# Convolution in a four-layer kernel: taps spread over four engines, and the transposed result stored by blocks of 32 rows

## The chip, the core and the metric

The kernel runs on one core of a Trainium2 chip, in one launch. The metric is device time in microseconds. A core has a matrix engine (TensorE, PE in the profile), a vector engine (VectorE, DVE), an activation engine (ScalarE, ACT), a general engine (GpSimd, POOL) and a queue that here only issues DMAs (SyncE, SP). They run side by side and wait for each other by semaphores. TensorE writes to PSUM, an accumulator memory of eight banks, each of which holds one 128x512 float32 tile; other data is in SBUF, the on-chip memory with 128 partitions, or in DRAM.

## What is computed

Four layers on an image of 256x256 positions with 128 channels, in float32, each of the form `x = x + layer(group_norm(x))`. The change touches layer 1, a selective state-space scan in four directions. Its start, cut from the reference:

```python
xz = x @ w_in.T
xi, z = jnp.split(xz, 2, axis=-1)                    # xi: 256 inner channels
xc = jnp.transpose(xi, (0, 3, 1, 2))
xc = depthwise_conv3x3(xc, conv_w) + conv_b          # one 3x3 filter per channel
xc = silu(xc)
x_flat = xc.reshape(b, d, L)                         # row by row
x_t = jnp.transpose(xc, (0, 1, 3, 2)).reshape(b, d, L)   # column by column
x_hwwh = jnp.stack([x_flat, x_t], axis=1)
xs = jnp.concatenate([x_hwwh, jnp.flip(x_hwwh, axis=-1)], axis=1)
```

The four sequences in `xs` (by rows, by columns, and both backwards) then each go through a projection, a softplus, and a recurrence over all 65536 positions with 16 states per channel.

## The kernel before

`program` runs a pass for the statistics and then the layers one after the other. Layer 1 (`layer1`) is three stages: `conv_block` (the convolution), `scan_stream` (the scan, by far the longest part of the whole kernel) and `scan_end`.

**The convolution.** The inner channels are two halves of 128 (`dh`), which lie on the partitions. The image is cut into 16 blocks of 16 rows; a block and a half make a *part*, 32 parts in all, numbered `i`. Each part has eight *units* `u` of two rows, so a unit is a tile of 128 channels by 512 positions, and there are 256 units. A unit passes through these steps:

- `products` (line 472): some of the nine taps on TensorE. Since projecting and filtering are both linear, the projection's weights are multiplied by the tap's weights beforehand (`taps`, line 434), and one matrix product from the normalised input `xps` gives projection and tap at once, summed into the PSUM tile `l1a_mm`. A float32 product stands in the trace as two records.
- `rest` (line 487): the other taps on VectorE. Each is one instruction (line 493) that multiplies a shifted window of the projected input `l1a_xi` in SBUF by a weight per channel and adds it to `l1a_mm`.
- `silu` (line 502): two ScalarE instructions read the finished tile, one (line 511) into `l1a_o`, row by row, the other (line 512) into `l1a_ot`, a tile of 256 columns by 32 rows in which neighbouring rows of one column are neighbours.

`on_pe` (line 420) names the taps on TensorE: four of the nine in even units, three in odd ones. So VectorE does five taps or six, in turns.

`inner_x` (line 457) makes `l1a_xi` for the next part: one product with the plain projection weights into `l1a_pi` (two PSUM banks) and one ScalarE copy (line 471) for each of the nine pairs of rows. At its start VectorE clears the borders of a new `l1a_xi` (line 462); there are two such buffers, so that this waits for the last tap of the part before. `load_x` and `norm_x` (lines 439 and 453) bring the next block of input into `l1a_xp`, in two DMAs, and normalise it on VectorE (line 455).

The loop (line 536) writes out the order by hand, and every engine takes its instructions in that order: at unit `n` come `products(n)`, `rest(n-1)`, `inner_x` of the next part, and `silu(n-3)`. The pool of `l1a_mm` has five PSUM banks, so TensorE can be ahead of `silu` by that many units.

**What is stored.** For every 8 rows `l1a_o` goes to the DRAM tensor `l_xc`, by rows, and for every 32 rows `l1a_ot` goes to `l_xct`, by columns (line 521). `l_xct` is laid out as 256 channels by 65536 positions with whole columns in a run, so that 32 rows of a column are a run of 128 bytes, and one store has 32768 of them.

**The scan.** `scan_stream` takes the four directions `k` one after the other, each in 128 chunks of 512 positions. For a pair of chunks one block `l1b_xc` of 1024 positions and both halves is loaded from `l_xc` (k = 0 and 2) or `l_xct` (k = 1 and 3), by one DMA (line 625). It is read by TensorE for the projection (`xproj`, line 643) and, in the first two directions, for the start of the output sum (`y_start`, line 793), and by VectorE in `delta_x` (line 717), which multiplies step sizes in PSUM by `x`. The bulk of a chunk is sixteen recurrences on VectorE (line 769), with products on VectorE and GpSimd (lines 736 and 784), and loads of the spread-out `b` and `c` (lines 663 and 669). The outputs `y` of the directions by columns already have a layout by blocks of 32 rows, `[256, S // 32, S, 32]`; `in_block` and `block_dma` (lines 596 and 604) address such a block, which has runs of 32 elements in SBUF and of 512 bytes in DRAM.

Between convolution and scan stand the loads of the scan's weights (`scan_weights`, line 891); all these DMAs, stores and loads alike, are issued by SP, in the program's order.

Of the kernel before, what the change touches and what calls it, by code (L numbers as in the profile page):

```python
# [413 lines left out]
def conv_block(c, x1, ab, xc, xct):  # L414

    tc, nc, t = c.tc, c.nc, c.t
    R, RO, RT = 16, 8, 32
    on_pe = ((0, 2, 6, 8), (0, 2, 6))  # L420
    NU = R // 2
    parts = [(b, dh) for b in range(S // R) for dh in range(2)]
    with ExitStack() as a:
# [3 lines left out]
        wk = a.enter_context(tc.tile_pool(name="l1a_wk", bufs=2))  # L427
        ps = a.enter_context(tc.tile_pool(name="l1a_ps", bufs=5, space=PSUM))
        psi = a.enter_context(tc.tile_pool(name="l1a_pi", bufs=2, space=PSUM))
# [6 lines left out]
        cb = load(nc, one, t["l1_convb"], "l1a_cb")  # L436
        xps, raw, xis, mms, os_, ots = {}, {}, {}, {}, {}, {}

# [34 lines left out]
        def products(i, u):  # L473
            b, dh = parts[i]
            r = 2 * u
            mm = mms[i, u] = ps.tile([P, 2, S], F32, name="l1a_mm")
            for n, tap in enumerate(on_pe[u % 2]):
                dy, dx = divmod(tap, 3)
                nc.tensor.matmul(
                    mm,  # L480
                    taps[:, tap, dh * P : dh * P + P],
                    xps[b][:, r + dy : r + dy + 2, dx : dx + S],
                    start=n == 0,
                    stop=n == len(on_pe[u % 2]) - 1,
                )

        def rest(i, u):
            dh, r, mm = parts[i][1], 2 * u, mms[i, u]
            for tap in range(9):
                if tap in on_pe[u % 2]:  # L490
                    continue
                dy, dx = divmod(tap, 3)
                nc.vector.scalar_tensor_tensor(  # L493
                    mm,
                    xis[i][:, r + dy : r + dy + 2, dx : dx + S],
                    each[:, dh, tap : tap + 1],
                    mm,
                    ALU.mult,
                    ALU.add,
                )  # L500

        def silu(i, u):
# [17 lines left out]
            if rt == RT - 2:  # L520
                nc.sync.dma_start(
                    xct[ds_].rearrange("p (w h) -> p w h", h=S)[:, :, h1 - RT : h1], ots.pop(dh)
                )

# [9 lines left out]
        for r in range(NU + 1):  # L534
            inner_x(0, r)
        for n in range(len(parts) * NU + 3):
            i, u = divmod(n, NU)
            if i % 2 == 0 and i + 2 < len(parts) and u in (1, 5, 7):
                if u == 1:
                    load_x(parts[i + 2][0])  # L540
                else:
                    norm_x(parts[i + 2][0], u // 7)
            late(products, n)
            late(rest, n - 1)
# [7 lines left out]
def scan_stream(c, xc2, y, w):  # L552
# [18 lines left out]
    with ExitStack() as a:  # L571
# [31 lines left out]

        def block_dma(k, i, yo, store):
            b = i * CH // BL
            if k % 2 == 0:
                pairs = [(y[k][:, bass.ts(b, BL)].rearrange("(h p) t -> p h t", p=P), yo)]
            else:
                pairs = [
                    (  # L610
                        y[k][h * P : h * P + P, :, bass.ts(b, NW)].rearrange("p b w r -> p b (w r)"),
                        yo[:, h].rearrange("p (b m) -> p b m", m=NW * R),
                    )
                    for h in range(2)
                ]
            for far, near in pairs:
                nc.sync.dma_start(*((far, near) if store else (near, far)))

        def load_x(ch):

            if ch >= N:
                return
            k, i = chunks[ch]
            xc = io.tile([P, 2, BL], F32, name="l1b_xc")
            nc.sync.dma_start(
                xc, xc2[k % 2][:, bass.ts(i * CH // BL, BL)].rearrange("(h p) t -> p h t", p=P)
            )
            blocks[ch] = blocks[ch + 1] = [xc, None]

        def load_y(ch):  # L630
# [4 lines left out]
            if k >= 2:  # L635
                block_dma(k - 2, i, yo, False)

        def xproj(ch):
# [3 lines left out]
            for dh in range(2):  # L642
                nc.tensor.matmul(  # L643
                    du1[:40],
                    w["xproj"][:, dh, k, :],
                    blocks[ch][0][:, dh, cols(ch)],
                    start=dh == 0,
# [66 lines left out]
        def delta_x(ch, dh):  # L714
            if ch >= N:
                return
            nc.vector.tensor_tensor(  # L717
                du1 if dh else mm, mm, blocks[ch][0][:, dh, cols(ch)], ALU.mult
            )
# [67 lines left out]
        def y_start(ch, dh):  # L787
# [4 lines left out]
            else:  # L792
                nc.tensor.matmul(
                    ys[dh], w["dsum"][:, k, dh], xc[:, dh, cols(ch)], start=True, stop=False
                )
# [11 lines left out]
        def y_out(ch, dh):  # L807
# [3 lines left out]
            yo = blocks[ch][1]  # L811
            got = ys[dh] if k % 2 == 0 else ys[dh].rearrange("p (w b r) -> p w b r", b=S // R, r=R)
            nc.scalar.copy(in_block(yo, ch, dh), got)
            if dh == 1 and ch % 2 == 1:
                block_dma(k, i, yo, True)

# [282 lines left out]
def layer1(c, x1, x2p, x2, ab, stats):  # L1099
    tc = c.tc  # L1100
    with ExitStack() as ctx:
        dram = ctx.enter_context(tc.tile_pool(name="l1_dram", bufs=1, space=DRAM))
        xc = dram.tile([256, NPOS], F32, name="l1_xc")
        xct = dram.tile([256, NPOS], F32, name="l1_xct")
        shapes = [256, NPOS], [256, S // 32, S, 32]
        y = [dram.tile(shapes[k % 2], F32, name=f"l1_y{k}") for k in range(4)]
        conv_block(c, x1, ab, xc, xct)
# [612 lines left out]
```

## Time and profile before

| | us |
|---|---|
| three timed runs, median (lowest to highest) | 34541.69 (34539.79 to 34548.45) |
| the profiled execution's own time | 34537.54 |
| its span, first to last instruction | 34535.8 |
| busy in the span: VectorE, TensorE, GpSimd, ScalarE | 31354.0, 29222.5, 26717.0, 22500.8 |
| convolution, first tap product to last silu | 1146.4 |
| scan, start of the first recurrence to the end of the last | 25569.2 |

The profile is of one execution. It gives, for groups of like instructions, the source line, the engine, the operation, the tile written and the tiles read, shapes, count, busy time and mean length of one in ns, and the idle time before them with what ended it. A wait is put down to the instruction whose semaphore ended it. The granted clock (PEclk) is the share of full speed that TensorE was given in a stretch; in the windows it stands behind the engines' busy times, and DMA behind it is the mean busy share of the 16 DMA engines. A timeline line is start, length, engine, line, operation, and how many like instructions it merges.

### The profile page before, as it was taken

What the parts mean: (1) busy time and instruction counts of PE and PEld (TensorE: products, weight loads), DVE (VectorE), ACT (ScalarE), POOL (GpSimd) and SP (SyncE); (2) the same over time, 40 slices, a digit from 0 to 9 for tenths busy, and PEclk for the clock granted to TensorE, in tenths of its full rate; (3) what the DMA queues carried; (4) which work ended last, traced back from release to release, by engine and by line L of the source; (5) the groups of instructions that cost most, each with busy time, mean ns of one, the idle gap of its engine ahead of it and who ended that gap; (6) DMA issues with size and microseconds to landing.
All of it is one profiled execution on the core that took longest, in us unless ns stands there. A gap on an engine that the chain in (4) does not pass through costs nothing. (4 is left out here: it accounts for less than half of the span.)

```text
span 34535.8 us, 255681 instructions
## 1 busy us (share of the span) xinstructions
PE 29222.5 (85%) x72564; PEld 12231.8 (35%) x72564; DVE 31354.0 (91%) x24089; ACT 22500.8 (65%) x46445; POOL 26717.0 (77%) x6484
## 2 busy tenths in 40 slices
PE   7999888888888888888888888888888888899888
PEld 2554333333333333333333333333333333334444
DVE  5668899999999999999999999999999999863699
ACT  3665577777777777777777777777777777532476
POOL 2441199999999999999999999999999999620000
PEclk8999999999999999999999999999999999999888
DMA  3113655555555555555555555555555555674111
GB/s 136 45 45 99 155 190 190 191 191 191 189 191 191 190 190 192 191 190 191 195 201 200 202 201 199 202 204 200 201 202 200 201 202 202 213 236 147 66 34 33
DMA packets 2367335, 5947.80 MB, mean 172 GB/s; under 512 B 637447, under 2 KB 1639704, under 8 KB 1792086
## 3 DMA queue, kind: packets, MB, share of 16 engines
q1 hardware_dynamic: 2230742, 5864.31, 47.6%
q10 hardware_dynamic: 135168, 67.13, 0.6%
q8 instruction: 572, 9.37, 0.1%
q14 instruction: 853, 6.99, 0.1%
HBM read 5238.41 MB, written 692.58 MB: 172 GB/s over the span
## 5 line engine op out<-in xcount | busy, mean ns | idle before, releaser
L769 DVE TENSOR_TENSOR_SCAN l1b_h<-l1b_da,l1b_state,l1b_db 128x1024 f32<-128x1024 f32 x8192 | 18793.1, 2336 | 596.1 <-ACT l1b_db L758 583.8
L784 POOL TENSOR_TENSOR l1b_hc<-l1b_h,l1b_cc 128x2048 f32<-128x2048 f32 x4096 | 18446.0, 4528 | 329.2 <-DVE l1b_h L769 328.4
L803 PE MATMUL l1b_y<-l1b_hc,ident 128*128 128x512 f32 x32768 | 16052.8, 639 | 1117.9 <-POOL l1b_hc L784 1117.8
L754 ACT ACTIVATE l1b_da<-l1b_dl,l_A 128x512 f32<-128x512 f32 (+1 forms) x16384 | 11297.5, 690 | 3156.7 <-DVE l1b_h L769 2848.5
L803 PEld LDWEIGHTS l1b_y<-l1b_hc,ident 128*128 128x128 f32 x32768 | 6524.5, 205 | 10687.1 <-issue 8157.6
L736 POOL TENSOR_TENSOR l1b_db<-l1b_bb,l1b_dus 128x2048 f32<-128x2048 f32 x1536 | 6966.8, 4536 | 1245.2 <-DMA l1b_bb<-l1b_bc 1245.2
L736 DVE TENSOR_TENSOR l1b_db<-l1b_bb,l1b_du 128x2048 f32<-128x2048 f32 x2048 | 4658.4, 2275 | 35.2
L758 ACT ACTIVATE l1b_db<-l1b_state,l1b_db,l1b_af 128x1 f32<-128x1 f32 x8192 | 3045.1, 372 | 0.0
L675 PE MATMUL l1b_mm<-l1b_xd,l_dtw 41*128 41x512 f32 x2048 | 1374.6, 756 | 1714.1 <-ACT l1b_dus L725 1708.3
L701 PE MATMUL l1b_mm<-l1b_tail,ident 128*128 128x512 f32 x2048 | 1292.2, 717 | 1388.4 <-ACT l1b_tail L695 1388.4
L780 ACT COPY l1b_state<-l1b_h 128x4 f32<-128x4 f32 x4095 | 789.7, 193 | 2433.5 <-DVE l1b_h L769 2433.4
L326 POOL TENSOR_TENSOR l0b_e<-l0b_e,l0b_den 128x1024 f32<-128x1024 f32 x512 | 969.0, 1893 | 1403.0 <-DVE l0b_den L325 784.3
L701 PE MATMUL l1b_mm<-l1b_relu,ident 128*128 128x512 f32 x2048 | 1307.4, 727 | 0.0
L675 PEld LDWEIGHTS l1b_mm<-l1b_xd,l_dtw 41*128 41x128 f32 x2048 | 338.0, 206 | 2528.5 <-ACT l1b_dus L725 2131.4
L725 ACT COPY l1b_dus<-l1b_mm 128x512 f32<-128x512 f32 x512 | 299.6, 585 | 1388.2 <-DVE l1b_db L736 1387.7
L736 DVE TENSOR_TENSOR l1b_db<-l1b_bb,l1b_mm 128x2048 f32<-128x2048 f32 x512 | 1171.5, 2288 | 18.2 <-ACT l1b_dus L725 0.7
L302 DVE CUSTOM_DVE_ANT_0 l0b_e<-l0b_sc,l0b_bias 128x256 f32<-128x256 f32 x2048 | 745.5, 420 | 419.0 <-PE l0b_sc L291 415.7
L701 PEld LDWEIGHTS l1b_mm<-l1b_tail,ident 128*128 128x128 f32 x2048 | 377.1, 207 | 2059.0 <-ACT l1b_tail L695 1814.6
L493 DVE SCALAR_TENSOR_TENSOR l1a_mm<-l1a_xi,l1a_each,l1a_mm 128x512 f32<-128x512 f32 x1408 | 1046.1, 755 | 59.1 <-issue 13.0
L643 PE MATMUL l1b_du<-l1b_xc,l_xproj 128*40 128x512 f32 x2048 | 981.5, 602 | 62.4 <-DMA l_xproj<-in_l_xproj 58.8
L317 ACT ACTIVATE l0b_e<-l0b_e,l0b_top 128x256 f32<-128x256 f32 x2048 | 1012.2, 498 | 1.9 <-DVE l0b_top L302 1.9
L709 ACT COPY l1b_dl<-l1b_mm 128x512 f32<-128x512 f32 x1024 | 587.5, 574 | 524.5 <-DVE l1b_du L717 517.0
(256 smaller groups left out, 28744.8 us busy)
## 6 DMA issues: line engine op xcount, KB each, us to landing
l1b_bb<-l1b_bc SPq DMA_DIRECT2D x2048, 1024.0 KB
l1b_cc<-l1b_bc SPq DMA_DIRECT2D x2048, 1024.0 KB
l1b_xc<-l_xc SPq DMA_DIRECT2D x128, 1024.0 KB
l_y<-l1b_yo SPq DMA_DIRECT2D x128, 1024.0 KB
l1b_xc<-l_xct SPq DMA_DIRECT2D x128, 1024.0 KB
l_y<-l1b_yo SPq DMA_DIRECT2D x256, 512.0 KB
l_xc<-l1a_o SPq DMA_DIRECT2D x64, 1024.0 KB
l_xct<-l1a_ot SPq DMA_DIRECT2D x16, 4096.0 KB
```

Source lines behind the costliest of these rows:

```text
L317: nc.scalar.activation(e[:, i], e[:, i], AF.Exp, scale=-1.0, bias=top[:, i : i + 1], accum_out=den[:, i : i + 1],)
L326: nc.gpsimd.tensor_tensor(e, e, den[:, :, None].to_broadcast([P, 4, S]), ALU.mult)
L493: nc.vector.scalar_tensor_tensor(mm, xis[i][:, r + dy : r + dy + 2, dx : dx + S], each[:, dh, tap : tap + 1], mm, ALU.mult, ALU.add,)
L643: nc.tensor.matmul(du1[:40], w["xproj"][:, dh, k, :], blocks[ch][0][:, dh, cols(ch)], start=dh == 0, stop=dh == 1,)
L675: nc.tensor.matmul(mm, w["dt"][:, chunks[ch][0], dh * P : dh * P + P], xds[ch % 3][0:41], start=True, stop=True,)
L701: nc.tensor.matmul(mm, c.ident, part, start=i == 0, stop=i == 1)
L736: eng.tensor_tensor(db, bbs[g // 2], du[:, None, :].to_broadcast([P, G, CH]), ALU.mult)
L754: nc.scalar.activation(da[:, o + lo : o + hi], dl[:, lo:hi], AF.Exp, scale=w["A"][:, k, dh, n : n + 1])
L758: nc.scalar.activation(first, states[k][:, dh, two : two + 1], AF.Identity, scale=af[:, two : two + 1], bias=first,)
L769: nc.vector.tensor_tensor_scan(h_, a_, d_, states[k][:, dh, one : one + 1], ALU.mult, ALU.add)
L784: nc.gpsimd.tensor_tensor(hc, hs[g], ccs[g // 2], ALU.mult)
L803: nc.tensor.matmul(ys[j % 2], c.ident, hc[:, i], start=False, stop=j // 2 * G + i == 15)
```

## The change

Taps 0, 2 and 6 are on TensorE in every unit. Taps 1 and 7 go to ScalarE in every unit: each is an activation with the identity function and the weight as scale, into a tile of its own in SBUF. Tap 4 goes to GpSimd in even units. GpSimd sums these two or three products into one tile (`l1a_t`), and VectorE, which does the other three or four taps as before, adds that tile to `l1a_mm` once. The new step `three` is called at the head of a unit's turn, for the unit after it. The pool of `l1a_mm` gets a sixth bank.

`l_xct` takes the layout by blocks of 32 rows that `y` has, so that a store of `l1a_ot` writes 32 KB in a run for each channel. In exchange, a block of it is loaded by two DMAs with runs of 512 bytes, and lies in SBUF in runs of 32 elements, which the readers of `l1b_xc` follow.

```diff
-    R, RO, RT = 16, 8, 32
-    on_pe = ((0, 2, 6, 8), (0, 2, 6))
+    R, RO, RT = 16, 8, xct.shape[3]
+    on_pe = 0, 2, 6
+    on_act, on_pool = (1, 7), 4
...
-        ps = a.enter_context(tc.tile_pool(name="l1a_ps", bufs=5, space=PSUM))
+        ps = a.enter_context(tc.tile_pool(name="l1a_ps", bufs=6, space=PSUM))
...
-            for n, tap in enumerate(on_pe[u % 2]):
+            for n, tap in enumerate(on_pe):
...
+        def window(i, u, tap):
+            dy, dx = divmod(tap, 3)
+            return xis[i][:, 2 * u + dy : 2 * u + dy + 2, dx : dx + S]
+
+        def three(i, u):
+            dh = parts[i][1]
+            for j, tap in enumerate(on_act):
+                t_ = sums[i, u, j] = wk.tile([P, 2, S], F32, name=f"l1a_t{j}", bufs=3)
+                nc.scalar.activation(
+                    t_, window(i, u, tap), AF.Identity, scale=each[:, dh, tap : tap + 1]
+                )
+            t_ = sums[i, u] = wk.tile([P, 2, S], F32, name="l1a_t", bufs=3)
+            one_, two = sums.pop((i, u, 0)), sums.pop((i, u, 1))
+            if u % 2 == 0:
+                nc.gpsimd.tensor_scalar(
+                    t_, window(i, u, on_pool), each[:, dh, on_pool : on_pool + 1], None, ALU.mult
+                )
+                nc.gpsimd.tensor_tensor(t_, t_, one_, ALU.add)
+                one_ = t_
+            nc.gpsimd.tensor_tensor(t_, one_, two, ALU.add)
 
         def rest(i, u):
-            dh, r, mm = parts[i][1], 2 * u, mms[i, u]
+            dh, mm = parts[i][1], mms[i, u]
             for tap in range(9):
-                if tap in on_pe[u % 2]:
+                if tap in on_pe or tap in on_act or tap == on_pool and u % 2 == 0:
                     continue
...
                 nc.vector.scalar_tensor_tensor(
...
+                    mm, window(i, u, tap), each[:, dh, tap : tap + 1], mm, ALU.mult, ALU.add
+                )
+            nc.vector.tensor_tensor(mm, mm, sums.pop((i, u)), ALU.add)
...
-                nc.sync.dma_start(
-                    xct[ds_].rearrange("p (w h) -> p w h", h=S)[:, :, h1 - RT : h1], ots.pop(dh)
-                )
+                nc.sync.dma_start(xct[ds_, h1 // RT - 1], ots.pop(dh))
...
+        three(0, 0)
         for n in range(len(parts) * NU + 3):
...
+            late(three, n + 1)
             late(products, n)
             late(rest, n - 1)
...
+        def like_block(ap, ch):
+
+            if chunks[ch][0] % 2 == 0:
+                return ap
+            return ap.rearrange("p (w b r) -> p w b r", b=S // R, r=R)
...
             xc = io.tile([P, 2, BL], F32, name="l1b_xc")
-            nc.sync.dma_start(
-                xc, xc2[k % 2][:, bass.ts(i * CH // BL, BL)].rearrange("(h p) t -> p h t", p=P)
-            )
+            block_dma(xc2[k % 2], k, i, xc, False)
...
-                    blocks[ch][0][:, dh, cols(ch)],
+                    in_block(blocks[ch][0], ch, dh),
...
             nc.vector.tensor_tensor(
-                du1 if dh else mm, mm, blocks[ch][0][:, dh, cols(ch)], ALU.mult
+                like_block(du1 if dh else mm, ch),
+                like_block(mm, ch),
+                in_block(blocks[ch][0], ch, dh),
+                ALU.mult,
             )
...
-                    ys[dh], w["dsum"][:, k, dh], xc[:, dh, cols(ch)], start=True, stop=False
+                    ys[dh], w["dsum"][:, k, dh], in_block(xc, ch, dh), start=True, stop=False
...
-        xct = dram.tile([256, NPOS], F32, name="l1_xct")
         shapes = [256, NPOS], [256, S // 32, S, 32]
+        xc = dram.tile(shapes[0], F32, name="l1_xc")
+        xct = dram.tile(shapes[1], F32, name="l1_xct")
```

## The prediction

> **What bounds the kernel now.** I read the windows first, cut at the borders of the stages that the diff touches: the convolution (first tap product to last silu), the passage from it to the scan, and the scan's four passes, from each pass's first recurrence (L769) to the next's, the last to the end of its last.
>
> ```profile
> core 0: us, PE busy (x) PEld busy (x) DVE busy (x) ACT busy (x) POOL busy (x), PEclk, DMA share, GB/s
> 2952.10:4098.50 1146.40, 1054.55 (x2351) 455.98 (x2349) 1090.36 (x1483) 580.03 (x793) 0.00 (x0) 0.95 0.61 141
> 4098.50:4176.80 78.30, 19.78 (x22) 4.79 (x22) 11.07 (x19) 11.16 (x20) 4.50 (x1) 0.57 0.78 197
> 4176.80:10571.80 6395.00, 5344.10 (x10737) 2091.24 (x10738) 6232.59 (x2946) 4505.84 (x9217) 6307.40 (x1408) 0.92 0.51 190
> 10571.80:16966.80 6395.00, 5349.50 (x10757) 2092.66 (x10757) 6232.49 (x2947) 4503.62 (x9213) 6313.64 (x1409) 0.92 0.52 191
> 23361.90:29746.00 6384.10, 5331.97 (x10721) 2087.19 (x10722) 6224.38 (x2940) 4494.87 (x9194) 6312.00 (x1407) 0.92 0.55 200
> ```
>
> In the convolution VectorE is busy 95% of 1146.4 us, TensorE 92%, ScalarE half, GpSimd not at all. In the scan VectorE (97%) and GpSimd (99%) set the pace. Next the convolution's groups and its waits:
>
> ```profile
> L493 DVE SCALAR_TENSOR_TENSOR l1a_mm<-l1a_xi,l1a_each,l1a_mm 128x512 f32<-128x512 f32 x1408 | 1046.1, 755 | 59.1 <-issue 13.0 <-PE l1a_mm L479 4.5
> L479 PE MATMUL l1a_mm<-l1a_xp,l1a_taps 128*128 128x512 f32 x1792 | 851.5, 617 | 73.3 <-ACT l1a_ot L512 73.3
> L512 ACT ACTIVATE l1a_ot<-l1a_mm,l1a_cb 128x512 f32<-128x512 f32 x256 | 294.7, 1151 | 0.0
> ```
>
> ```profile
> ACT l1a_xi L471 <- DVE l1a_xi L462: 119.0, 16, 8.2
> ACT l1a_xi L471 <- DVE l1a_xp L443: 41.1, 14, 3.5
> DVE l1a_mm L493 <- PE l1a_mm L479: 4.5, 10, 0.6
> ```
>
> VectorE waits for TensorE 4.5 us in all: it is the bound, and the taps on it (5.5 a unit, a unit being one 128x512 tile, 256 units) are what costs. Last the timeline, for start-to-start times, since consecutive instructions overlap:
>
> ```profile
> 3206.67 33.96 DVE L493 SCALAR_TENSOR_TENSOR l1a_mm<-l1a_xi,l1a_each,l1a_mm 128x512 f32<-128x512 f32 x44 [0.29 <-issue]
> ...
> 3147.80 3.60 PE L479 MATMUL l1a_mm<-l1a_xp,l1a_taps 128*128 128x512 f32 x8
> ...
> 5011.35 0.63 ACT L695 ACTIVATE l1b_tail<-l1b_tail 128x512 f32<-128x512 f32 x1
> 5011.89 1.40 ACT L754 ACTIVATE l1b_da<-l1b_dl,l_A 128x512 f32<-128x512 f32 x2
> 5013.22 0.37 ACT L758 ACTIVATE l1b_db<-l1b_state,l1b_db,l1b_af 128x1 f32<-128x1 f32 x1
> ```
>
> Eight units of VectorE taps take 33.96 us, 0.77 each; in the trace a tap following another on its own tile starts 0.79 after it, one on a new tile 0.66 after. Eight TensorE records, four taps, end 3.60 after the first starts: one per 0.43 ((3.60-0.59)/7) at full clock.
>
> **VectorE's part.** It loses two taps a unit and gains one addition: three taps and an addition in even units, four and an addition in odd. The addition reads PSUM and one SBUF tile, as L717 does in the scan: 0.674 long; beginning the next tile's work behind it costs what it costs behind a tap now, about 0.09 less than its length, 0.58 (0.71 if it hides nothing, as L717 in the scan). A unit is 3.5 x 0.79 + 0.58 = 3.35 (3.48), plus the normalisation L455, 32 times 1.52 over 256 units = 0.19, plus memsets 0.02: 3.56, or 911 us (945 with the dearer addition). The same sum for before gives 4.5 x 0.79 + 0.66 + 0.21 = 4.43, 1133 us against the 1146.4 seen, so it holds to about 1%.
>
> **TensorE's part.** Three taps are 6 records, the inner product (9 per 8 units) 2.25: 8.25 x 0.43 = 3.54 us a unit instead of 3.97. All units: 906 us at full clock; at the granted 0.95 of this stage, 954. That is above VectorE's 911, so TensorE becomes the bound.
>
> **ScalarE's part.** It adds two Identity activations a unit, SBUF to SBUF, scaled by a column. Nearest rows: L695 (SBUF to SBUF, next start 0.54 later) and L754 (scaled by a column, into PSUM, 1.33 for two): 0.54 to 0.665. 580 + 512 x that = 856 to 920 us; I take 0.6, 887, nearer the first row because the destination is SBUF. Its order per unit is two Identities, one inner copy, two silus. The 160 us of waits at part starts (119.0 + 41.1) are ScalarE arriving early; busy 77% more, it arrives later, and they shrink.
>
> **GpSimd's part.** One scalar multiply and three additions per pair of units. Per element: L784 4528 ns for 2048 makes 1.13 us for an addition, L191 1195 for 1024 makes 0.60: 4.0 us a pair, 511 us in all. The dearest 128x512 addition in the trace, L961 with strided input, takes 1.56: 4 x 1.56 = 6.2 a pair, still under TensorE's 7.4. So it is hidden. VectorE's last addition is a new wait: on GpSimd's sum, which needs ScalarE's two products. Behind it queue the next unit's taps, the normalisations and the memsets that ScalarE's copies wait for. But the products are issued two units before that addition, about 7 us for 1.3 + 2.9 of work, and buffers are three deep; I cost it at nothing. If the cover were gone, the price would be some 3 us at each of 32 part starts.
>
> GpSimd's work beside VectorE has one price that the trace shows, in the stage after the scan:
>
> ```profile
> 29902.35 1.79 DVE L1004 TENSOR_SCALAR l1c_xn<-l1c_x,ab 128x512 f32<-128x512 f32 x1
> ...
> 29900.83 3.02 POOL L961 TENSOR_TENSOR l1c_y<-l1c_y,l1c_yt 128x512 f32<-128x512 f32 x2 [8.02 <-DMA l1c_y<-l_y]
> ```
>
> That VectorE instruction has a median of 0.548 and took 1.79 while a GpSimd addition ran: up to 1.24 late. L455 is the same operation, so 32 x (0 to 1.13, one GpSimd addition) adds 0 to 36 us to VectorE, making it 911 to 947, still below TensorE. The taps and L717 read one SBUF operand, and L717 keeps 0.674 in the scan beside a GpSimd 99% busy: no price. The Trainium skill's page SBUF — State Buffer, "Who interferes with whom", warns that VectorE's 2-port modes and two-SBUF-input operations lock GpSimd out and are locked out by it, for a whole instruction. Applied to every VectorE instruction it would make the offload pointless; by its own limit to those modes and operand kinds it touches L455 alone.
>
> **The stage.** Three engines end near each other: 954, 911 to 947, 887. With hand-overs 1 to 3% above the largest I take 970 (930, where the clock is granted more, to 1020, where all three hold each other up). 1146.4 - 970 = 176 saved.
>
> **The transposed store.** Its 16 issues stay, with whole 32 KB rows instead of 128-byte runs. In the convolution this hides under VectorE; at the end it shows:
>
> ```profile
> 4099.19 35.40 SPq L48 DMA_DIRECT2D l_xproj<-in_l_xproj  x1
> ...
> 4145.34 0.56 ACT L655 COPY l1b_xd<-l1b_du 40x512 f32<-40x512 f32 x1
> ```
>
> SP is held 35.4 us at the first weight load behind the last store, whose drain runs at a flat 145 GB/s in the DMA view; the scan's first copy comes 46.8 us after the convolution's end. Long rows move at 350 to 430 GB/s in that view, so 4 MB take about 11 us, plus 1 MB of l_xc and some 4 us for loads and first products: copy at 15 to 22 us. Saved 25 to 32; I take 28, and keep 12 (200 GB/s, the slow patches between) to 34.
>
> **The scan.** Passes two and four load l_xct by 512-byte runs in two issues: 128 issues of 0.43 us more on SP, ahead of the b and c loads. The passes already say what such loads cost: the fourth loads and stores y like that, the second stores it, the first does neither, yet passes one and two are equal at 6395.0. Cost nothing, the cover being the prefetch of two chunks; without it, some 1 us x 128. VectorE's L717 reads runs of 32 elements, 512 times. ScalarE's L813 writes that pattern in passes two and four: 146.20 us for 256 instructions, against 145.05 for 254 contiguous ones in pass one, 0.571 each in both. Nothing; upper end in the third rival.
>
> **Sum.** 176 + 28 = 204 off the profiled execution's 34537.5 (span 34535.8): 34334. The median of the runs, 34541.7, lies 4 above: 34338.
>
> **Rivals.**
> *ScalarE takes over and keeps its waits.* For: 920 us at the dearer Identity, and 160 us of waits on VectorE's memset (up to 8.2 each), which is a true dependency. Against: those waits come from arriving early. 920 + 160 = 1080, saving 66 + 28: 34444. Chance 0.09.
>
> *GpSimd pays for alternating operations (slower).* No row of before shows a scalar multiply next to an addition. Two switches a pair; GpSimd decides from 1.7 us a switch ((7.4 - 4.0) / 2), the kernel is slower from 2.6 ((9.0 + 0.2 - 4.0) / 2, 9.0 being the pair now and 0.2 the 28 us shared out). At 4.36, the gap before L191 that the timeline most often puts down to issue, the stage is 128 x (4.0 + 8.72) = 1628: 34338 + 658 = 34996. Against: the only two pool configurations of the whole trace stand ahead of L191, though multiplies, additions and copies follow. Chance 0.05. The skill's GPSIMD Engine Reference, "Instruction dispatch", puts some 6 us on the first call to a freshly loaded kernel; paid at each switch, that would be an estimated 2048 us for the stage, and no row here shows it.
>
> *The strided read costs in the scan.* The dearest stride in the trace is L512 against L511, 1151 against 692 ns for 4-byte steps: 0.46 x 512 = 235 us on VectorE, which has no slack there: 34573, no change. Against: L813. Chance 0.03.
>
> **How the numbers follow.** The forecast has 0.83; its own range is a stage of 930 to 1020, a passage of 12 to 34 and 0 to 15 us of strided reads, 34288 to 34419. To leave out no more than 0.2, the range takes the first rival in: 34290 to 34450. 0.2% of this kernel is 69 us, about what its measurement tells from no change. Forecast and first rival (0.92) are faster by more, less 0.05 for mixtures that fall short: 0.87. Same: the third rival and most of the mixtures, 0.07. Slower: 0.06.
>
> **What would show it.** Right: convolution 930 to 1020 us; TensorE busiest there, with VectorE waiting for l1a_mm from TensorE; Identity pitch 0.54 to 0.67; GpSimd additions near 1.13; first L655 copy 15 to 22 us after the last silu; passes within 2 us of 6395. Wrong: GpSimd above 7 us a pair, ScalarE over 95% busy, VectorE waiting for l1a_t, or a second and fourth pass longer than the first.

## The result, and the profile after

| | before | after |
|---|---|---|
| median of the runs, us (lowest to highest) | 34540.74 (34534.36 to 34548.45) | 34313.07 (34306.94 to 34318.44) |
| ratio, 95% interval | | 0.9934 (0.9921 to 0.9946) |
| the profiled execution's own time, its span | 34537.54, 34535.8 | 34318.44, 34316.7 |
| convolution, first tap product to last silu | 1146.4 | 940.0 |
| from there to the first recurrence | 78.3 | 53.3 |
| four passes of the scan | 25569.2 | 25569.4 |
| from the end of the last recurrence to the end of the span | 4789.7 | 4804.1 |

The kernel became 228 us faster, 0.66%. Between the two profiled executions lie 219.1 us: 206.4 in the convolution, 25.0 in the passage, 2.3 ahead of both, and 14.4 lost again after the scan. That last number is not the change's. The stage after the scan, whose code is the same in all kernels here, took between 1045.3 and 1059.3 us (first to last instruction on a tile of its own) in the eleven executions profiled, and the profile after happens to hold the longest.

The windows of the changed kernel, cut as those of before, so that they can be laid line beside line (the passage is the second row, the first two passes of the scan the last two):

```profile
core 0: us, PE busy (x) PEld busy (x) DVE busy (x) ACT busy (x) POOL busy (x), PEclk, DMA share, GB/s
2949.80:3889.80 940.00, 909.83 (x2095) 392.19 (x2093) 884.53 (x1227) 837.68 (x1306) 712.67 (x511) 0.99 0.45 176
3889.80:3943.10 53.30, 20.09 (x22) 4.80 (x22) 11.06 (x19) 11.12 (x20) 4.50 (x1) 0.56 0.62 245
3943.10:10338.20 6395.10, 5343.21 (x10737) 2090.76 (x10738) 6232.43 (x2945) 4505.95 (x9218) 6307.34 (x1408) 0.92 0.51 190
10338.20:16733.00 6394.80, 5353.14 (x10757) 2093.28 (x10757) 6232.59 (x2946) 4503.63 (x9213) 6313.69 (x1409) 0.92 0.53 191
```

In the convolution four engines now are busy 76 to 97% of the time, and the granted clock rose from 0.95 to 0.99. The scan did not move. Next the convolution's groups. The lines are shifted: L515 are VectorE's taps (L493 before), L518 its addition, L481 TensorE's taps, L497 the Identity activations, L503 GpSimd's multiply, L506 and L508 its additions, L529 and L530 the silus.

```profile
L481 PE MATMUL l1a_mm<-l1a_xp,l1a_taps 128*128 128x512 f32 x1536 | 701.2, 593 | 6.7 <-ACT l1a_ot L530 6.7
L515 DVE SCALAR_TENSOR_TENSOR l1a_mm<-l1a_xi,l1a_each,l1a_mm 128x512 f32<-128x512 f32 x896 | 674.1, 752 | 32.9 <-PE l1a_mm L481 10.2
L497 ACT ACTIVATE l1a_t<-l1a_xi,l1a_each 128x512 f32<-128x512 f32 x512 | 356.1, 795 | 0.0
L508 POOL TENSOR_TENSOR l1a_t<-l1a_t,l1a_t 128x512 f32<-128x512 f32 x256 | 324.5, 1273 | 110.8 <-ACT l1a_t L497 100.7
L503 POOL TENSOR_SCALAR l1a_t<-l1a_xi,l1a_each 128x512 f32<-128x512 f32 x127 | 227.3, 1789 | 56.8 <-DVE l1a_xi L464 26.0 <-ACT l1a_t L497 22.5 <-DVE l1a_mm L518 8.3
L518 DVE TENSOR_TENSOR l1a_mm<-l1a_mm,l1a_t 128x512 f32<-128x512 f32 x256 | 179.2, 700 | 27.4 <-POOL l1a_t L503 0.5 <-DVE l1a_mm L515 0.5
```

The waits of the same stretch (engine, tile and line that waited, what ended it; total us, times, longest):

```profile
ACT l1a_xi L473 <- DVE l1a_xi L464: 72.4, 16, 5.2
PE l1a_mm L481 <- ACT l1a_ot L530: 6.7, 14, 0.5
DVE l1a_mm L515 <- PE l1a_mm L481: 10.2, 2, 9.9
DVE l1a_mm L518 <- POOL l1a_t L503: 0.5, 1, 0.5
```

VectorE waits for TensorE twice (one is the stage's first tap, 9.9) and for GpSimd's sum once, 0.5 us. So nothing upstream holds it up, and by busy time alone (884.53 against TensorE's 909.83) one would still not call it the bound. The timeline says why it is: a tap is 0.75 long, but the next tap on the same tile starts 0.79 after it, and the addition 0.86 after the last tap. These pauses are not busy time. The lines show an odd unit's four taps between two even units' three (start, length, and how many like instructions in a row):

```profile
3049.92 2.33 DVE L515 SCALAR_TENSOR_TENSOR l1a_mm<-l1a_xi,l1a_each,l1a_mm 128x512 f32<-128x512 f32 x3
3052.36 0.70 DVE L518 TENSOR_TENSOR l1a_mm<-l1a_mm,l1a_t 128x512 f32<-128x512 f32 x1
3052.97 3.12 DVE L515 SCALAR_TENSOR_TENSOR l1a_mm<-l1a_xi,l1a_each,l1a_mm 128x512 f32<-128x512 f32 x4
3056.20 0.70 DVE L518 TENSOR_TENSOR l1a_mm<-l1a_mm,l1a_t 128x512 f32<-128x512 f32 x1
3056.80 2.33 DVE L515 SCALAR_TENSOR_TENSOR l1a_mm<-l1a_xi,l1a_each,l1a_mm 128x512 f32<-128x512 f32 x3
```

From the first tap of one unit to that of the next, an even unit takes 3052.97 - 3049.92 = 3.05 us and an odd one 3.83, with no wait in them: 3.44 in the mean, plus 0.21 for the normalisation and 0.02 for memsets, 3.67 x 256 = 939. That is the stage.

At the stage's end, SP's first weight load and the scan's first copy (L655 before):

```profile
3890.22 1.21 SPq L48 DMA_DIRECT2D l_xproj<-in_l_xproj  x1
...
3911.24 0.56 ACT L677 COPY l1b_xd<-l1b_du 40x512 f32<-40x512 f32 x1
```

SP is no longer held (1.21 us instead of 35.40), and the copy comes 21.4 us after the last silu instead of 46.8.

### The profile page after: what moved, and what is told of

It reads as the page before. It is cut to its first block, busy times and chain, and to the rows that moved or that the text cites. A ratio compares the mean times of both kernels' runs of the same rounds, so it can differ in the third digit from the quotient of the medians.

```text
span 34316.7 us, 256885 instructions
## 1 busy us (share of the span) xinstructions
PE 29098.7 (85%) x72308; PEld 12172.7 (35%) x72308; DVE 31152.4 (91%) x23833; ACT 22759.1 (66%) x46957; POOL 27431.3 (80%) x6996
## 5 line engine op out<-in xcount | busy, mean ns | idle before, releaser
L761 POOL TENSOR_TENSOR l1b_db<-l1b_bb,l1b_dus 128x2048 f32<-128x2048 f32 x1536 | 6965.0, 4535 | 46.9 <-DMA l1b_bb<-l1b_bc 46.9
L985 POOL TENSOR_TENSOR l1c_y<-l1c_y,l1c_yt 128x512 f32<-128x512 f32 x256 | 394.7, 1564 | 606.6 <-DMA l1c_y<-l_y 527.1
```

The source lines that it names most:

```text
L761: eng.tensor_tensor(db, bbs[g // 2], du[:, None, :].to_broadcast([P, G, CH]), ALU.mult)
```

## Experiments

### The new layout without the new taps

From the kernel before: only the storing, loading and reading of `l_xct` as in the change. The store's lines, the rest left out:

```diff
-                nc.sync.dma_start(
-                    xct[ds_].rearrange("p (w h) -> p w h", h=S)[:, :, h1 - RT : h1], ots.pop(dh)
-                )
+                nc.sync.dma_start(xct[ds_, h1 // RT - 1], ots.pop(dh))
...
```

> The taps as before, only the transposed result stored and loaded by blocks of 32 rows. My theory: the convolution stays at 1146 us with a granted clock of 0.95, since VectorE's taps set its pace and TensorE still has waits of some 5 us; the first scan copy comes 21 to 22 us after the last silu instead of 46.8; the passes stay at 6395. In all 25 us less than before. Rival (the 128-byte stores slow the convolution too, through DMA load or stalls of SP): the convolution is more than 10 us shorter, or its clock rises.

Measured: 34519.66 us against 34543.16 beside it, ratio 0.9993 (0.9984 to 1.0003). That is 24 us less, with each of its ten runs below each of the seventeen beside it, but by the interval not told from nothing. The profile places it: the convolution took 1147.5 us (1146.4 before) at a clock of 0.95 as before, the first copy came 21.3 after the last silu instead of 46.8, the passes stayed at 6395.1. What follows: in the convolution at the old pace the store was hidden, as the prediction said, and the drain at its end was worth 25.5 us (28 in the sum).

### The new taps without the new layout

The changed kernel with `l_xct` stored, loaded and read as before.

> The taps as after, the transposed result stored and loaded as before. My theory: the convolution takes 940 to 945 us at a granted clock of 0.98 or more, because TensorE's long waits are gone with the taps; SP is held some 35 us behind the last store and the first scan copy comes 47 us after the last silu. In all 206 us less than before. Rival (the clock of the convolution follows the DMA load or chance, not TensorE's own waits): the clock is 0.95 again, TensorE needs 906/0.95 = 954 us and the convolution takes 955 to 970.

Measured: 34441.56 us, ratio 0.9971 (0.9960 to 0.9982), 102 us less than before, and 128 more than with both parts. Convolution 1031.7 us (940.0 with both parts), passage 95.0 (53.3). What was expected for it missed: alone the parts bring 24 and 102, together 228. The rival's clock of 0.95 came, but not for the rival's reason: it stands behind 14 stops of TensorE of 2.9 to 8.4 us, each put down to ScalarE. The waits of the convolution, of which none of the DMA ones stands in the changed kernel's list:

```profile
ACT l1a_o L529 <- DMA l_xc<-l1a_o: 87.8, 12, 9.3
DVE l1a_xp L457 <- DMA l1a_xp<-x: 46.9, 7, 7.2
PE l1a_mm L481 <- ACT l1a_ot L530: 77.7, 22, 8.4
```

And SP's timeline (start, how long the issue took). The first and the last row are each the first issue of `l1a_o` behind a store of `l1a_ot`:

```profile
3193.56 19.03 SPq L535 DMA_DIRECT2D l_xc<-l1a_o  x1
...
3218.24 1.07 SPq L539 DMA_DIRECT2D l_xct<-l1a_ot  x1
...
3324.16 18.99 SPq L535 DMA_DIRECT2D l_xc<-l1a_o  x1
```

Behind a store in 32768 short runs, the next issue of the other store holds SP for 19 to 25 us: so at all 15 stores that another `l1a_o` follows, where in the changed kernel it takes 0.32 us at each. (A row of several issues in such a view, like the 41 us that the expectation for four `l1a_o` buffers starts from, also holds the time in which SP waits for ScalarE between them; in the changed kernel, where no issue is held, three of these issues span 31 us.) ScalarE then has no free `l1a_o` (87.8 us), VectorE no input (46.9), and a ScalarE that is late frees no PSUM, so TensorE waits for it (77.7). Before the change the next issue was held for 15 to 24 us and ScalarE waited for `l_xc` too, 27.0 us in all, but ScalarE was busy only half of the time and that lay in its slack. So on top of the new taps the layout is worth 128 us, not 24: 92 in the convolution and 42 in the passage, less some us that differ elsewhere.

### New taps, old layout, and four `l1a_o` buffers

```diff
-                os_[i] = wk.tile([P, RO, S], F32, name="l1a_o")
+                os_[i] = wk.tile([P, RO, S], F32, name="l1a_o", bufs=4)
```

> The taps as after, the old store of the transposed result, and four buffers instead of two for the row-wise result l1a_o. The taps alone had left the convolution at 1031 us, with 88 us of ScalarE waiting for a store of l1a_o and 47 us of VectorE waiting for input. My theory: SP issues in order and is held some 19 to 41 us behind each 128-byte store, so that the short stores and the loads behind it come late, though the queue has time left over (DMA busy 0.67): with four buffers ScalarE's 88 us go, the input's 47 us stay, and the convolution takes 960 to 990. Rival (the DMA engines can't move the stores at this pace at all): the convolution stays within 15 us of 1031 and the waits turn up elsewhere.

Measured, one run: 34414.1 us; convolution 998.4, which is 33 less than with two buffers and short of what was expected. ScalarE's wait for `l1a_o` is gone. Another has come, for `l1a_ot`, and VectorE's for its input is what it was:

```profile
ACT l1a_ot L530 <- DMA l_xct<-l1a_ot: 50.8, 14, 5.4
DVE l1a_xp L457 <- DMA l1a_xp<-x: 47.2, 7, 7.2
```

The issue behind each store is held for 19 to 29 us here. So the queue behind the short runs is late, not one buffer. Of the 92 us which the old layout costs this convolution, 33 are shown to be `l1a_o`; that the rest is the two waits above is not shown, since a third input buffer and a third `l1a_ot` were not tried.

### The kernel before, with three border-cleared input tiles

The prediction took the clock of 0.95 as a property of the stage. In the trace of before, TensorE's stops and its clock stand like this (timeline, then windows; PEclk is the last but two):

```profile
3060.53 1.02 PE L464 MATMUL l1a_pi<-l1a_xp,l1a_win 128*128 128x512 f32 x2
3066.52 5.81 PE L479 MATMUL l1a_mm<-l1a_xp,l1a_taps 128*128 128x512 f32 x8 [4.97 <-ACT l1a_ot L512]
```

```profile
3060.00:3066.50 6.50, 1.55 (x4) 0.38 (x2) 6.13 (x11) 2.23 (x4) 0.00 (x0) 0.81 0.00 0
3066.50:3070.00 3.50, 3.48 (x4) 1.52 (x5) 3.39 (x5) 2.00 (x3) 0.00 (x0) 0.50 0.00 0
3070.00:3073.40 3.40, 3.40 (x8) 1.47 (x7) 3.26 (x6) 0.18 (x1) 0.00 (x0) 0.88 0.00 0
```

With a stop of 4.97 us the clock goes to half for 6.8 us, of which 2.5 still lie in the stop, and the eight records behind it take 5.81 instead of 3.60. There are 15 such stops, of 3.8 to 4.97 us, one for every two parts; the clock is half for 3.4 us at the first, for 6.8 at the others, and once more in the stage's last 13.9 us, after TensorE's last product: (3.4 + 14 x 6.8 + 13.9) / 2 = 56 us of 1146, which is the 0.95. (Part of this half clock falls where TensorE has nothing to do, so that dividing all of its work by 0.95 overstates what it loses.) The stops come from ScalarE, whose copy into `l1a_xi` waits for VectorE's memset and holds up the silus behind it, so that no PSUM bank comes free. The experiment takes that wait's reason away: three fixed `l1a_xi` tiles, their borders cleared once.

```diff
+        fixed = [one.tile([P, R + 2, S + 2], F32, name=f"l1a_xi{j}") for j in range(3)]
+        for xi in fixed:
+            nc.vector.memset(xi[:, :, 0 : S + 2 : S + 1], 0.0)
...
-                xi = xis[i] = xi_.tile([P, R + 2, S + 2], F32, name="l1a_xi")
-                nc.vector.memset(xi[:, :, 0 : S + 2 : S + 1], 0.0)
+                xis[i] = fixed[i % 3]
```

> Before, with three fixed buffers for the projected input whose borders are cleared once, so that ScalarE's copies at a part's start no longer wait for VectorE. My theory: TensorE's waits of some 5 us (up to 5.8) disappear, only short ones for a PSUM bank remain, and the granted clock of the convolution rises from 0.95 to 0.98 or more; the stage stays within 5 us of 1146, because VectorE paces it. Rival (the clock drops for another reason: DMA load, or chance from execution to execution): the clock stays at 0.95. Second rival (TensorE paces the convolution before): the stage gets shorter by 20 us or more.

Measured, one run: 34528.91 us. The window of its convolution, and its one stop that still cost clock:

```profile
2945.00:4077.60 1132.60, 1039.26 (x2351) 435.50 (x2349) 1085.56 (x1453) 583.49 (x795) 0.00 (x0) 0.99 0.62 144
...
3136.00:3141.00 5.00, 4.88 (x8) 2.10 (x9) 4.79 (x8) 2.09 (x4) 0.00 (x0) 0.66 0.00 0
```

```profile
3136.12 4.54 PE L481 MATMUL l1a_mm<-l1a_xp,l1a_taps 128*128 128x512 f32 x6 [2.56 <-ACT l1a_ot L514]
```

The clock is 0.99: it followed the stops, while the DMA engines were as busy as before (0.62 against 0.61), which speaks against the rival of the DMA load. Yet the stage is only 14 us shorter, since VectorE set the pace before and TensorE's clock was all but off the path. (Less than 5 us had been expected. Of the 14, some 7 are the 30 memsets, which no longer stand between VectorE's taps: from tap to tap across one it was 0.89 us, without it 0.66. Some 6 are the steps in which VectorE waited for TensorE, 4.5 us of waits before and none now.)

### The changed kernel with VectorE's taps of two units in turns

If VectorE paces the changed kernel, shortening its chain must show, until TensorE takes over. The taps of units u - 1 and u are issued alternately, so that a tap does not follow another on its own tile, and `l1a_t` gets five buffers. `rest` then does both units at the odd one and nothing at the even one; `todo` lists the taps of the two:

```diff
...
+            for v in (u, u - 1):
+                left = [tap for tap in range(9) if tap not in on_pe and tap not in on_act]
+                todo.append([(v, tap) for tap in left if v % 2 or tap != on_pool])
+            for k in range(len(todo[0])):
+                for one_ in todo[:1] + (todo[1:] if k else []):
+                    v, tap = one_[k if one_ is todo[0] else k - 1]
+                    nc.vector.scalar_tensor_tensor(
+                        mms[i, v], window(i, v, tap), each[:, dh, tap : tap + 1], mms[i, v], ALU.mult, ALU.add
+                    )
...
```

> After, with VectorE's taps of two units in turns, so that an instruction seldom follows one on its own PSUM tile. My theory: VectorE paces the convolution after (3.67 us a unit by its start-to-start times); taps on another tile start 0.66 instead of 0.79 apart, so that a unit falls to some 3.2 us and TensorE's 906 us at full clock take over: stage 906 to 925, 15 to 34 us less than after. Rival (TensorE or ScalarE paces it already): the stage stays within 5 us of 940. Second rival (longer chains between the engines, since silu waits for two units): the stage gets longer.

Measured: 34287.77 us (34276.04 to 34292.84), ratio 0.9926 (0.9911 to 0.9941), 25 us under the changed kernel. Window and wait:

```profile
2950.00:3863.70 913.70, 900.82 (x2095) 394.58 (x2093) 835.32 (x1227) 839.85 (x1306) 710.55 (x511) 1.00 0.46 181
```

```profile
DVE l1a_mm L520 <- PE l1a_mm L481: 63.4, 66, 13.3
```

VectorE now waits for TensorE 63.4 us (10.2 before the edit), TensorE is busy 98.6% of the window, and its pauses add up to 1.0 us. VectorE's taps, when they follow one on another tile, start 0.66 after it. (The five buffers are a second difference; VectorE had waited for `l1a_t` for 0.5 us in all with three, so they can hardly be what brought it.) This is what the prediction had forecast for the change, TensorE as the bound; the stage had to become 26 us shorter to get there, and the price is 906 to 914, the "full clock" term, not 954.

### As above, with the scan's weights loaded ahead of the convolution

```diff
-        conv_block(c, x1, ab, xc, xct)
         with tc.tile_pool(name="l1_w", bufs=1) as wp:
-            tc.keep_in_program_order(c.nc.scalar.preload_act_table_set(EXP_LN))
             w = scan_weights(c, wp)
+            conv_block(c, x1, ab, xc, xct)
+            tc.keep_in_program_order(c.nc.scalar.preload_act_table_set(EXP_LN))
```

> The version with VectorE's taps of two units in turns, and the scan's weights loaded before the convolution instead of behind its last store. My theory: the weights' landing behind the 4 MB store sets the start of the scan (first scan copy 21 us after the last silu); with it gone the copy comes 5 to 9 us after the last silu, 12 to 16 us are saved, against 2 to 5 us more ahead of the convolution: 34275 to 34283. Rival (the scan's first x blocks, or the spread b and c, are as late): less than 5 us saved.

Measured: 34284.64 us, ratio 0.9927 (0.9911 to 0.9944): no difference to the version above. The weights are there, and the first copy still comes 20.3 us after the last silu. The scan's first product in the version above, and in this one:

```profile
3878.45 3.60 PE L671 MATMUL l1b_du<-l1b_xc,l_xproj 128*40 128x512 f32 x4 [26.63 <-DMA l_xproj<-in_l_xproj]
```

```profile
3886.05 3.23 PE L671 MATMUL l1b_du<-l1b_xc,l_xproj 128*40 128x512 f32 x4 [28.86 <-DMA l1b_xc<-l_xc]
```

The edit exchanged one wait for another. Above, the first two `l1b_xc` are issued 12 us ahead of the last store of `l1a_ot`, and the product waits for the weights behind that store, as the theory had it. Here the two `l1b_xc` are issued behind the store, and the product waits for them. What the passage would be with both ahead of the store is open.

### GpSimd's multiply in four forms

In the groups after stands 1789 ns for the multiply (median 1563), where the prediction took 0.60 us. To find what sets that price, the changed kernel gets another form in each of four parts: tap 4 as in the change, tap 3's window, contiguous fixed data, and that data with a second operation (an addition of a column). Only the first form computes tap 4, so the run is of use for times alone.

```diff
+                if i % 4 == 0:
+                    nc.gpsimd.tensor_scalar(t_, window(i, u, 4), one_w, None, ALU.mult)
+                elif i % 4 == 1:
+                    nc.gpsimd.tensor_scalar(t_, window(i, u, 3), one_w, None, ALU.mult)
+                elif i % 4 == 2:
+                    nc.gpsimd.tensor_scalar(t_, taps[:, 0:2, :], one_w, None, ALU.mult)
+                else:
+                    nc.gpsimd.tensor_scalar(t_, taps[:, 0:2, :], one_w, one_b, ALU.mult, ALU.add)
```

> After, with GpSimd's multiply in four forms by part: the window of tap 4 as it is; the window of tap 3 (one element to the left); 512 elements in one run of another tile; the same with a second operation, as the row had from which 0.60 us was taken. Only the first form is tap 4. After showed 1.56 us. My theory: the cost lies in the shape of the window, two runs of 256 with a gap: the two forms in one run take 0.6 to 0.75, both windows 1.56. Rival (the single-operation form is slow): only the fourth form is fast. Second rival (start address): the tap-3 window is faster than the tap-4 one. Third: with GpSimd as loaded as here, all four take 1.56.

One run: 34306.96 us, the convolution as after (939.9). Each form's durations (lowest, median, highest, in ns), from the views of the four lines:

```profile
L505 POOL TENSOR_SCALAR l1a_t<-l1a_xi,l1a_each x32: 1553/1561/2542, 2942.7 to 3787.8; 128x512 f32<-128x512 f32 x32
...
L509 POOL TENSOR_SCALAR l1a_t<-l1a_taps,l1a_each x32: 1556/1563/2540, 3004.0 to 3846.1; 128x512 f32<-128x512 f32 x32
...
L511 POOL TENSOR_SCALAR l1a_t<-l1a_taps,l1a_each,l1a_cb x32: 757/768/1776, 3033.5 to 3873.1; 128x512 f32<-128x512 f32 x32
```

Window or contiguous makes no difference (1561, 1563); the form with two operations takes half as long, 768. And the row from which the price had been taken is of that form, as its two columns of operands say:

```profile
L191 POOL TENSOR_SCALAR l0a_d<-l0a_d,l_gamma,l_beta x64: 1194/1195/1196, 125.7 to 542.5; 128x1024 f32<-128x1024 f32 x64
```

It multiplies by `gamma` and adds `beta`; the change's multiply has one column, `l1a_each`, and bears the same name TENSOR_SCALAR.

### Tap 4 on GpSimd in every unit, with one operation and with two

First the changed kernel with only this:

```diff
-            if u % 2 == 0:
+            if True:
...
-                if tap in on_pe or tap in on_act or tap == on_pool and u % 2 == 0:
+                if tap in on_pe or tap in on_act or tap == on_pool:
```

> After, with tap 4 on GpSimd in every unit, so that VectorE has three taps and the addition throughout (3.05 + 0.22 = 3.27 us a unit). My theory: GpSimd needs 1.655 + 1.35 + 1.25 = 4.26 us a unit by its start-to-start times and becomes the bound: convolution 1085 to 1110 us, VectorE waiting for l1a_t. By the prices that I took beforehand (0.60 and 1.13, 2.9 us a unit) TensorE would set it: 906 to 930.

Measured, one run: 34479.9 us, convolution 1116.4. The wait that had been costed at nothing:

```profile
DVE l1a_mm L518 <- POOL l1a_t L508: 311.3, 254, 1.3
```

GpSimd was busy 1056.64 of 1100 us inside the stage and set the pace. By the prediction's prices (0.60 + 2 x 1.13 a unit) it would have stayed under TensorE. Then the same with the multiply as two operations:

```diff
+        zero = one.tile([P, 1], F32, name="l1a_zero")
+        nc.gpsimd.memset(zero, 0.0)
...
-                    t_, window(i, u, on_pool), each[:, dh, on_pool : on_pool + 1], None, ALU.mult
+                    t_, window(i, u, on_pool), each[:, dh, on_pool : on_pool + 1], zero, ALU.mult, ALU.add
```

> The changed kernel with tap 4 on GpSimd in every unit, its multiply written as two operations (times the weight, plus a column of zeros). With the multiply as one operation this took 1117 us for the convolution, GpSimd busy 1056.6 us. Theory: the form sets the price. A multiply of two operations had a median of 0.77 us against 1.56, so GpSimd loses 256 x 0.79 = 202 us, falls to about 855 and is no longer the bound; VectorE has three taps and an addition in every unit, 3.05 + 0.23 = 3.28 us or 840 in all; TensorE with 906 to 913 is the longest: convolution 915 to 945 us, multiplies of 0.77, the kernel 34290 to 34320. Rival 1: the short multiplies were short because of what they read (fixed, contiguous weights) together with the form; then a two-operation multiply of the shifted window takes some 1.56 again and the convolution stays near 1117. Rival 2: the multiplies get shorter, but the chain product, multiply, two additions is too long for the distance at which it is issued, and VectorE still waits for the sum: convolution 960 to 1050.

Measured: 34293.08 us (34290.68 to 34296.66), ratio 0.9928 (0.9912 to 0.9945). Window of its convolution, the multiply's group, and VectorE's wait for the sum:

```profile
2948.90:3869.70 920.80, 903.60 (x2095) 394.07 (x2093) 784.34 (x1099) 844.22 (x1306) 875.39 (x767) 0.99 0.45 178
```

```profile
L505 POOL TENSOR_SCALAR l1a_t<-l1a_xi,l1a_each,l1a_zero 128x512 f32<-128x512 f32 x255 | 197.5, 774 | 0.0
```

```profile
DVE l1a_mm L520 <- POOL l1a_t L510: 105.0, 210, 0.5
```

A second operation, which computes nothing, takes 196 us from the stage (1116.4 to 920.8): 774 ns on the shifted window, in a kernel where each of GpSimd's multiplies is of this form. VectorE has a hundred us less work than in the changed kernel, and still the stage is no shorter than with its taps in turns (913.5). Two engines now run through almost without a pause: TensorE, whose pauses add up to 2.7 us, and GpSimd, busy 875.39 us, its next instruction mostly starting within 0.1 us of the last one's end. It is GpSimd's sum that VectorE waits for, at 210 of 256 units, against 12.9 us for TensorE, 9.9 of them at the first tap. So GpSimd sets the pace here, with TensorE just below it: the second rival's wait came, at a stage far below that rival's 960 to 1050.

## Why the prediction was right, and where it was not

**The time.** 34338 was forecast, 34313 measured. Against the profiled execution: 176 + 28 = 204 forecast; 206.4 + 25.0 measured in the two places, less the 14.4 after the scan that no step of the change explains. (The range's lower end, 34288, and the first rival's 34444 are counted from the profiled execution, the forecast and the upper end from the median, 4 us higher; that decides nothing.) That the forecast came so near is in part luck. The engine that was named as the bound was not it, and of the signs that were to show it right, "VectorE waiting for l1a_mm from TensorE" did not come: 10.2 us, 9.9 of them at the first tap. The stage stayed inside its 930 to 1020 because three engines were put near each other: VectorE, the true bound, came to 939, only 15 below the 954 that was wrongly put above it, and no hand-overs of 1 to 3% came on top.

**VectorE.** "3.56, or 911 us (945 with the dearer addition)" and 0 to 36 us for L455: 3.67 a unit and 939 were measured, inside that. The addition begins the next unit's work 0.61 behind it (0.58 taken, 0.71 the upper end), but is itself 0.86 behind the last tap (0.79 taken). L455, now L457, kept its median of 1.607 and reached 2.37 beside GpSimd; its mean of 1.83 makes (1.83 - 1.61) x 32 = 7 us. The taps, at 752 ns against 755 before, paid nothing. That speaks for the limit stated by the Trainium skill's page SBUF — State Buffer, "Who interferes with whom", which confines the locking to some forms of instruction; the taps beside a GpSimd that is busy 76% of the stage show it.

**TensorE: the step that failed.** "at the granted 0.95 of this stage, 954. That is above VectorE's 911, so TensorE becomes the bound." Its work was right (909.8 busy, 906 forecast at full clock, records 0.43 apart), the clock was not: 0.99, no stop over 0.9 us, no stretch at half clock before its last product. The 0.95 was no property of the stage but the trace of 15 stops, which the prediction saw from the other side ("ScalarE arriving early") and did not join with the clock. The experiment with three tiles shows the same without any new tap. (What took the stops out of the changed kernel itself, the later ScalarE or the sixth PSUM bank, was not tested apart; with the sixth bank and the old layout they are there.) So VectorE remained the bound, which the experiment that takes pauses from it and the one that takes work from it confirm, and the stage came out at 940 where 970 was taken.

**ScalarE.** 887 forecast, 837.7 busy. The Identity's step was 0.58 to 0.61, as taken; its length (795) and the silus' (773, 1242) rose, their steps did not. The sum is high because it took the 580 of before as they were: there the second silu, 1.15 long, was mostly followed by idle time, and now an Identity starts 0.94 after it, 256 x 0.21 = 54 us. ("Busy 77% more" does not come out of the prediction's own numbers: 580 to 887 is 53%.) Its waits at part starts fell from 160 to 91 us in all (72.4 and 18.8): they shrank, as forecast. The rival in which they stay in full did not come.

**GpSimd: two terms mis-sized, both hidden.** The multiply, 0.60 by L191, took 1.56; the addition, 1.13, took 1.27. GpSimd was busy 712.67 / 128 = 5.6 us a pair instead of 4.0, of the 7.3 that a pair has. "I cost it at nothing" held: 0.5 us. The second rival, a price for alternating, did not come: the addition behind a multiply (L506) takes 1273 ns like the one behind an addition (L508), and in the trace it starts 1.66 us after the multiply, 0.09 behind its end. The failing step is the choice of the row: L191 is another form. Tap 4 in every unit shows how near the edge was.

**The store.** "In the convolution this hides under VectorE" was right of the kernel before and is what the layout alone shows. It was the smaller half of the truth: at the new pace the old store costs 92 us in the convolution, and 128 in all. The prediction summed the two parts as if each kept its own worth, 176 and 28; alone they bring 102 and 24, and the sum came out because the part that depends on the other was in the change. The passage was as forecast, 21.4 of 15 to 22.

**The scan.** The passes moved by 0.3 us at most: the 128 more issues and the reads in runs of 32 cost nothing that can be seen. (L512, by which the third rival was priced, writes 4-byte elements 128 bytes apart; runs of 32 elements are far from that.)

## What to carry to other kernels

A granted clock under 1 in a busy stage is to be traced to TensorE's stops before it is multiplied into a forecast: what removes the stops gives the clock back. Two edits in one stage are not summed each at its own worth: a transfer hidden under the old bound must be laid under the new, shorter one. And a price is taken from a row with the same operands, not only the same name: what made that error harmless here was that GpSimd had every second unit free of the multiply. And moving one load ahead of a long store bought nothing where another that the next stage waits for fell behind it.

## What the hardware showed that was not expected

- TensorE's clock halves soon after a short stop, and a stop's length alone does not decide (ends of matmuls are modelled). With three input tiles a stop of 2.56 us went with 3.4 us at half clock, stops of 2.10 and 2.37 with none; with tap 4 on GpSimd in every unit 21 stops of 1.65 to 2.79 us did, and others of the same lengths, up to 2.80, did not; stops of 2.9 to 8.4 us went with 3.4, 6.8 or 10.2 us. In these convolutions every stretch at half clock is a whole multiple of 3.41 us long and begins a whole multiple of 3.41 us after another. The Trainium skill's TensorE: Matmul & The Clock Gate, "HAM oscillation — how this bites in real kernels", warns of stops over some 3.4 us; here less was enough.
- GpSimd's multiply by a column of weights on 128x512 takes 1.56 us as one operation and 0.77 as two.
- On VectorE a tap on the tile of the tap before starts 0.79 us after it, on another tile 0.66: 896 taps in turns brought 26 us.
- After a 4 MB store in runs of 128 bytes SP was held for 19 to 25 us by the next issue (0.32 with runs of 32 KB), and beside faster work the layout was worth 128 us.
